# Layer 0's bias: three DMA folds to four rows a key, one sum product a group, and VectorE evicting the fourth quarter in 3 of 16 quads

## The chip, the cores and the metric

The kernel runs on one core of a Trainium2 chip. Its engines have queues of their own and meet through semaphores: TensorE (PE in the profile; PEld is its weight load), VectorE (DVE), ScalarE (ACT), GpSimd (POOL) and SyncE (SP, which here only issues DMAs). TensorE writes to PSUM, which VectorE and ScalarE can read[...]. The metric is the device time of the whole kernel in microseconds, as the median of several runs; lower is better.

## The reference

Four layers follow each other; only layer 0's attention bias matters here. For 16 groups (2 batches x 8 heads), 64 sampled keys and 1024 queries each, a small network turns the distance of query and key into one number that is added to the attention's logits:

```python
pos = grid_q[:, :, None, :] - grid_kv[:, None, :, :]
bias = jnp.sign(pos) * jnp.log1p(jnp.abs(pos))
bias = jax.nn.relu(bias @ cpb_w1 + cpb_b1)      # 2 -> 128
bias = jax.nn.relu(bias @ cpb_w2 + cpb_b2)      # 128 -> 128
bias = (bias @ cpb_w3 + cpb_b3)                 # 128 -> 1
...
sim = jnp.einsum('bhid,bhjd->bhij', qh, kh) + bias
attn = jax.nn.softmax(sim, axis=-1)
out = jnp.einsum('bhij,bhjd->bhid', attn, vh)
```

All is float32. The 16 x 64 x 1024 evaluations of the 128 x 128 product make up most of the kernel's matmul work.

## The kernel before

`layer0` walks over `quads`: `(u, o, half)` with `u` the group (0 to 15), `o` the pair of quads in it (0 to 7) and `half` 0 or 1. A quad is four keys, so 16 quads make a group's 64 keys and there are 256 quads in all. The text below calls `o` the pair.

*First hidden layer* (`first_hidden`, line 706, VectorE): for each of the four keys of a quad one tile of 128 hidden units x 1024 queries, an addition of an x part and a y part with a clamp at zero. It is issued one quad ahead, and its buffers hold two quads, so the tiles of quad i + 2 are written when TensorE is done with quad i.

*Second hidden layer* (`second_hidden`, line 730, TensorE): the 128 output units are sorted once (`sorted_weights`) so that units with like signs of `cpb_w3` stand together, and the weights' sizes are worked into the matrix. They are computed in four quarters of 32 units. A quarter's PSUM tile `hp` holds 4 keys x 32 units on its 128 partitions and all 1024 queries; three such tiles take turns. ScalarE evicts each with a bias and relu (line 740). What remains of the third layer is a sum with signs over 128 units:

- quarter 0 is multiplied by a sign per row (line 742, ScalarE), then added to quarter 1 by an accumulating DMA that GpSimd issues (line 747);
- quarter 3 += quarter 2 on GpSimd (line 751);
- quarter 3 += quarter 1 on GpSimd (line 754, in `join`, which runs during the next quad after its line 747).

That leaves 32 rows a key. Two quads share one tile `both` (`two_tiles`, three buffers). A first DMA fold (line 756, in `join` after the pair's second quad) adds odd rows to even ones: 16 rows a key. A second one (line 766, `refold`) leaves 8 rows a key; it runs in the second quad of the next pair, ahead of line 751. Right behind it SP copies (line 768) gather the rows of four quads in a tile of 16 keys x 8 rows (`sum`, three buffers). Two such tiles hold half a group; one product with a matrix of signs (`twice_product`, line 786, TensorE) sums the rows of both and puts 32 keys into the PSUM tile `sim`. It comes after pairs 5 and 1, two pairs after the last of its rows was computed. The last half group is treated apart, with one fold or none, to end early.

After a group's second product come its attention steps (`attend`): the keys' product (line 812), softmax on VectorE and ScalarE, and the values' product. The next pair of heads' preparation (`offsets`, `sampled`) is started at pair 1 of even groups. Both are generators: after each quad one step of attention runs, and, unless that step takes the turn for itself, one step of preparation.

The order on TensorE, ScalarE, VectorE and GpSimd is the order in which the loop issues (`manual_schedule`): for quad i the first layer of quad i + 1, the second layer of quad i with its evictions, then the steps.

Of the kernel before, what the change touches and what calls it, by code (L numbers as in the profile page):

```python
# [11 lines left out]
F32 = mybir.dt.float32  # L12
AF = mybir.ActivationFunctionType
ALU = mybir.AluOpType
# [21 lines left out]
    ("index", 1), ("row", 1), ("twelves", 8),  # L36
# [12 lines left out]
N_TWICE, N_FOLDED, N_SINGLE = 48, 56, 60  # L49
# [7 lines left out]
class Net:  # L57
# [40 lines left out]
    def layer0(self):  # L98
# [3 lines left out]
        with ExitStack() as ctx:  # L102
# [44 lines left out]
            with self.tc.manual_schedule(engines=engines):  # L147
# [39 lines left out]
                self.join, self.refolds, summed, group, sums = None, [], None, [], []  # L187
                for i, (u, o, half) in enumerate(quads):
                    self.half = half
                    if o == 1 and half == 1 and u % 2 == 0 and u // 2 + 1 < BP:  # L190
                        nxt = pairs[u // 2 + 1]
                        front += [self.offsets(nxt, u // 2 + 1, ps), self.sampled(nxt, u // 2 + 1, ps)]
                    h1 = ready
                    if i + 1 < len(quads):
                        if quads[i + 1][1:] == (7, 0) and u + 1 < 2 * BP:
                            self.advance(front, lambda: "logs" in pairs[(u + 1) // 2])
                        ready = self.first_hidden(*quads[i + 1], pairs, tables)
                    last_set = i >= len(quads) - 8
                    if half == 0:
                        if i + 2 < len(quads):  # L200
                            both = self.two_tiles(f"h2_{u}_{o}3")
                            group.append([both[:, 0, :], both[:, 1, :], both])
                        else:
                            group.append([self.four_rows(f"h2_{u}_{o}{n}3") for n in range(2)])
                        if o % 4 < 2 and not last_set:
                            sums.append(self.four_rows(f"sum{u}_{o}"))
                    self.second_hidden(i, u, o, half, h1, group[-1], i + 1 == len(quads), last_set)
                    if half == 1 and not last_set:
                        self.refolds.append((i + 2, group[-1][2], sums[o % 2], o % 4 // 2))
                    if half == 1 and o % 4 == 1 and summed:  # L210
                        v, e, zs = summed
                        self.twice_product(v, e, zs, sims, ps_s)
                        summed = None
                        if e == 1:
                            if v == 8:
                                self.advance(after, lambda: False)
                                att = [apool.tile([P, N], F32, tag=f"att{t}", name=f"att{v}_{t}") for t in range(CT)]
                            self.advance(front, lambda: "v" in pairs[v // 2])
                            after.append(self.attend(v, pairs[v // 2], sims.pop(v), att, ps))
                            if v % 8 == 7:  # L220
                                after.append(self.projection(ps, att, ow, v // 8))
                    elif half == 1 and o % 4 == 3:
                        if last_set:
                            self.folded_product(u, o - 2, group[:2], sims)
                        else:
                            summed, group, sums = (u, o // 4, sums), [], []
                    if not self.step(after):
                        self.step(front)

                self.join(True)  # L230
                self.advance(after, lambda: False)
                self.folded_product(u, o, group[2:3], sims)
# [35 lines left out]
    def sorted_weights(self, keep):  # L268
# [8 lines left out]
        self.places = self.spare[:, 3 * P : 4 * P + N_TWICE + N_FOLDED + N_SINGLE]  # L277
# [13 lines left out]
        many = keep.tile([P, 8], F32, tag="many", name="sort_many")  # L291
        vec.tensor_tensor(many, self.colr("twelves", 8), total.to_broadcast([P, 8]), ALU.is_le)
        vec.tensor_reduce(c["groups"], many, AX.X, ALU.add)
        vec.tensor_scalar(c["late"], c["groups"], 12.0, None, ALU.mult)
        vec.tensor_scalar(c["rest"], c["groups"], -12.0, 96.0, ALU.mult, ALU.add)
# [16 lines left out]
        signed = keep.tile([P, N_TWICE + N_FOLDED + N_SINGLE], F32, tag="signed", name="signed")  # L312
        pool.tensor_scalar(signed, self.places[:, P:], c["sign"], 1.0, ALU.mult, ALU.mult)
        self.twice = signed[:, 0:N_TWICE]
        self.folded = signed[:, N_TWICE : N_TWICE + N_FOLDED]
        self.single = signed[:, N_TWICE + N_FOLDED :]
# [15 lines left out]
        nc.scalar.copy(self.magb, small)  # L332
        self.flip = keep.tile([P, 1], F32, tag="flip", name="flip")
# [383 lines left out]
    def second_hidden(self, i, u, o, half, h1, one, final, last_set):  # L717

        nc = self.nc
        ys = []
        for q in range(4):
            hp = self.ps_h.tile([P, N], F32, tag="ps", name=f"hp_{u}_{o}{half}{q}")
            for h in range(2):
                cut = slice(h * HF, (h + 1) * HF)
                for k in range(4):
                    rows = slice(32 * k, 32 * k + 32)
                    nc.tensor.matmul(  # L730
                        hp[rows, cut], lhsT=self.l0w2[:, 32 * q : 32 * q + 32], rhs=h1[k][:, cut], start=True, stop=True
                    )
            if q < 3:
                y = self.hid2.tile([P, N], F32, tag=f"h2{q}", bufs=(2, 3, 2)[q], name=f"h2_{u}_{o}{half}{q}")
            else:
                y = one[half]
                if self.refolds and self.refolds[0][0] <= i:
                    self.refold(*self.refolds.pop(0)[1:])
            ys.append(y)
            nc.scalar.activation(y, hp, AF.Relu, bias=self.magb[:, q, 0:1])  # L740
            if q == 0:
                nc.scalar.activation(y, y, AF.Copy, scale=self.flip)  # L742
            elif q == 1:
                if final:
                    nc.vector.tensor_tensor(y, y, ys[0], ALU.add)
                else:
                    nc.gpsimd.dma_start(y, ys[0], accum_op=ALU.add)  # L747
                if self.join:
                    self.join(final)
            elif q == 3:  # L750
                (nc.vector if final else nc.gpsimd).tensor_tensor(y, y, ys[2], ALU.add)  # L751

        def join(final, z=ys[3], other=ys[1], fold=half == 1 and not final):
            (nc.vector if final else nc.gpsimd).tensor_tensor(z, z, other, ALU.add)  # L754
            if fold:
                nc.gpsimd.dma_start(one[2][0::2], one[2][1::2], accum_op=ALU.add)  # L756
                if last_set:
                    nc.sync.dma_start(one[0][1::2, :], one[1][0::2, :])

        self.join = join  # L760

    def refold(self, both, to, second):


        nc = self.nc
        nc.gpsimd.dma_start(both[0::4], both[2::4], accum_op=ALU.add)  # L766
        for half in range(2):
            nc.sync.dma_start(to[2 * second + half :: 4, :], both[0::4, half, :])

    def twice_product(self, u, e, zs, sims, ps_s):  # L770

        if u not in sims:
            sims[u] = ps_s.tile([P, HF], F32, tag="sim", name=f"sim{u}")
        at = 16 - 16 * e
        self.sum_product(u, self.twice[:, at : at + 32], e == 0, zs, sims)

    def folded_product(self, u, o, group, sims):
        at = 24 - 4 * (o - o % 2)  # L780
        self.sum_product(u, self.folded[:, at : at + 32], False, [one[0] for one in group], sims)

    def sum_product(self, u, lhsT, start, zs, sims):
        for h in range(2):
            for jj, z in enumerate(zs):
                self.nc.tensor.matmul(
                    sims[u][h * NJ + jj * 32 : h * NJ + jj * 32 + 32, :],
                    lhsT=lhsT,
                    rhs=z[:, h * HF : (h + 1) * HF],
                    start=start,  # L790
                    stop=False,
                )
# [1245 lines left out]
def _places():  # L2038

    q, row = np.arange(P) // 32, np.arange(P) % 32  # L2040
    got = np.zeros((P, P + N_TWICE + N_FOLDED + N_SINGLE), np.float32)
    got[:, :P] = np.where(q == 0, 96 + row, 12 * (row // 4) + 4 * (q - 1) + row % 4)
    p = np.arange(P)
    got[p, P + 16 + 8 * (p // 2 % 2) + 4 * (p % 2) + p // 32] = 1
    got[p, P + N_TWICE + 24 + 4 * (p % 2) + p // 32] = 1
    got[p, P + N_TWICE + N_FOLDED + 28 + p // 32] = 1
# [3 lines left out]
def _layout(i):  # L2050
# [10 lines left out]
    def over(v):  # L2061
# [13 lines left out]
        "row": (np.arange(P) % 32 // 4).astype(np.float32).reshape(P, 1), "twelves": over(np.arange(12, 108, 12, dtype=np.float32)),  # L2075
# [46 lines left out]
```

## Time and profile before

| what | value |
|---|---|
| median of 3 runs | 3223.9 us (3221.39 to 3224.66) |
| the profiled execution | 3223.45 us, its span 3221.7 us |
| bias stage, first to last start of line 730 | about 23 to 1902 us of the span |
| granted TensorE clock | 1.00 in every stretch |
| line 706, VectorE, first layer | 1020 of 128x1024, 1215 ns each |
| line 742, ScalarE, sign of quarter 0 | 256, 1152 ns each |
| line 747, GpSimd issue of the accumulating DMA | 255, 1080 ns each |
| lines 756 and 766, GpSimd issues of the folds | 127 of 859 ns, 124 of 1134 ns |
| line 768, SP copies, issue to landing | 248 of 128 KB, 3.5 us median |
| line 786, TensorE, sum products | 260 matmul records, 248 of them from copied rows |
| DMA queue of GpSimd | 232.82 MB, 37.4% of 16 engines over the span |

The profile is of one execution. A group in it is `line engine op out<-in shapes xcount | busy us, mean ns of one | idle us just before, and what ended it`. A float32 matmul is two records, and records of different column quarters run at once, so their durations must not be added; starts and the evictions that wait for them show the pace. Time in front of a DMA's landing is not in the issuing engine's busy time.

### The profile page before, as it was taken

The page shows a single profiled execution, that of the slowest core. Times are in us where ns is not written, and L with a number is a line of the kernel's source. Part 1 is how long each engine was busy: PE and PEld are TensorE (multiplying, and loading weights), DVE is VectorE, ACT ScalarE, POOL GpSimd, SP SyncE. Part 2 cuts the span into 40 slices and gives each one's busy share as a digit, 9 for nine tenths or more (in the row PEclk, how much of TensorE's full clock was granted, in tenths as well). Part 3 has the DMA queues.
Part 4 walks back from the last instruction along what each step waited for, and adds up shares of the span by engine and source line. Part 5 has one row for each costly group of instructions (what it writes and reads, how often), then busy time and mean ns, then how long its engine had stood idle before and what let it go on. Part 6 is the DMA issues. An engine that isn't in the chain of part 4 may idle for free.

```text
span 3221.7 us, 58840 instructions
## 1 busy us (share of the span) xinstructions
PE 3206.4 (100%) x24188; PEld 1218.9 (38%) x24188; DVE 2365.0 (73%) x2746; ACT 1958.2 (61%) x2032; POOL 2359.2 (73%) x1558
## 2 busy tenths in 40 slices
PE   9999999999999999999999999999999999999999
PEld 4343333333333333333333334444555433455333
DVE  7778788778777778878777765475475689755897
ACT  7887887887886687887887752112231566213662
POOL 6999999999998699998999964442343458634575
PEclk9999999999999999999999999999999999999999
DMA  6787877787786577777787762111000000000001
GB/s 178 163 172 158 171 168 163 166 167 165 162 172 145 124 164 161 163 163 164 163 174 160 166 166 79 39 40 39 1 1 12 29 1 1 15 1 14 1 2 54
DMA packets 94350, 341.90 MB, mean 106 GB/s; under 512 B 16624, under 2 KB 18800, under 8 KB 78896
## 3 DMA queue, kind: packets, MB, share of 16 engines
q0 software_dynamic: 52832, 232.82, 37.4%
q1 hardware_dynamic: 40224, 103.06, 10.0%
q8 instruction: 195, 3.19, 0.4%
q10 hardware_dynamic: 1008, 2.08, 0.2%
q14 instruction: 91, 0.75, 0.1%
HBM read 67.36 MB, written 4.46 MB: 22 GB/s over the span
## 4 chain that ended last, share of the span: by engine, by line
PE 90%; DVE 5%; POOL 2%; DMA 1%; issue 1%; ACT 0%; DVEq 0%; SPq 0%; POOLq 0%; ACTq 0%
PE hp L730 52%; PE s L1659 5%; PE o L1688 5%; PE qk20P L1434 2%; PE qk30P L1434 2%; PE qk31P L1434 1%; PE m_7P L943 1%; PE m_6P L943 1%; PE m_4P L943 1%; PE m_3P L943 1%; PE m_0P L943 1%; PE qk21P L1434 1%; PE m_5P L943 1%; PE m_2P L943 1%; PE m_1P L943 1%; DVE sum L1675 1%
## 5 line engine op out<-in xcount | busy, mean ns | idle before, releaser
L730 PE MATMUL hp<-h,w2s 128*32 128x512 f32 x16384 | 1784.1, 593 | 0.2
L706 DVE CUSTOM_DVE_ANT_1 h<-tx,bank 128x1024 f32<-128x1024 f32 (+1 forms) x1028 | 1180.9, 1211 | 295.7 <-PE hp L730 197.6
L740 ACT ACTIVATE h<-hp,magb 128x1024 f32<-128x1024 f32 x1024 | 1131.2, 1109 | 359.6 <-PE hp L730 357.7
L730 PEld LDWEIGHTS hp<-h,w2s 128*32 128x32 f32 x16384 | 559.3, 110 | 1187.0 <-issue 1126.4
L754 POOL TENSOR_TENSOR h<-h,h 128x1024 f32<-128x1024 f32 x254 | 728.2, 2867 | 2.4 <-DMA h<-h 2.3
L751 POOL TENSOR_TENSOR h<-h,h 128x1024 f32<-128x1024 f32 x255 | 717.4, 2814 | 1.5 <-ACT h L740 1.5
L1663 ACT ACTIVATE e<-s 128x1024 f32<-128x1024 f32 x256 | 261.8, 1024 | 181.0 <-PE s L1659 176.5
L747 POOL DMA_DIRECT2D h<-h x255 | 275.4, 1080 | 99.6 <-ACT h L740 97.7
L742 ACT ACTIVATE h<-h,flip 128x1024 f32<-128x1024 f32 x256 | 295.0, 1152 | 8.4
L1688 PE MATMUL o<-e,v 64*64 64x512 f32 x2048 | 265.3, 590 | 2.1 <-DVE q L1727 2.1
L1659 PE MATMUL s<-q,k 64*64 64x512 f32 x2048 | 266.0, 591 | 0.0
L1670 POOL TENSOR_TENSOR some<-some,e 128x1024 f32<-128x1024 f32 x64 | 167.6, 2619 | 26.7 <-ACT e L1663 24.1
L1668 POOL TENSOR_TENSOR some<-e,e 128x1024 f32<-128x1024 f32 x32 | 76.1, 2377 | 141.4 <-DVE sum L1677 106.3
L766 POOL DMA_DIRECT2D h<-h x124 | 140.6, 1134 | 27.0 <-DMA h<-h 24.6
L1675 DVE TENSOR_TENSOR sum<-sum,e 128x1024 f32<-128x1024 f32 x64 | 124.0, 1937 | 29.5 <-ACT e L1663 26.8
L913 POOL TENSOR_TENSOR mlp_w<-mlp_w 128x512 f32<-128x512 f32 x16 | 24.2, 1514 | 160.4 <-DMA mlp_w<-in_mlp_w 96.0
L756 POOL DMA_DIRECT2D h<-h x127 | 109.1, 859 | 38.9 <-POOL h L754 37.2
L1688 PEld LDWEIGHTS o<-e,v 64*64 64x64 f32 x2048 | 77.9, 133 | 144.9 <-issue 135.1
L1659 PEld LDWEIGHTS s<-q,k 64*64 64x64 f32 x2048 | 76.5, 133 | 133.2 <-issue 117.2
L1009 ACT ACTIVATE mh<-mh,cols 128x512 f32<-128x512 f32 x64 | 46.0, 721 | 124.4 <-DVE mh L1027 64.3
L1422 POOL TENSOR_TENSOR sq<-q 128x512 f32<-128x512 f32 x32 | 33.2, 1039 | 98.0 <-DVE q L1441 54.3
L1673 DVE TENSOR_TENSOR sum<-e,e 128x1024 f32<-128x1024 f32 x32 | 80.8, 2524 | 32.0 <-ACT e L1663 32.0
(583 smaller groups left out, 3254.4 us busy)
## 6 DMA issues: line engine op xcount, KB each, us to landing
h<-h POOLq DMA_DIRECT2D x382, 512.0 KB, 5.6
lb<-logs SPq DMA_DIRECT2D x63, 512.0 KB, 6.5
h<-h POOLq DMA_DIRECT2D x124, 256.0 KB, 3.7
sum<-h SPq DMA_DIRECT2D x248, 128.0 KB, 3.5
mlp_w<-in_mlp_w SPq DMA_DIRECT2D x16, 1024.0 KB, 4.9
x<-in_x SPq DMA_DIRECT2D x8, 512.0 KB, 7.8
qkw<-in_l_qk SPq DMA_DIRECT2D x2, 2048.0 KB, 7.9
out<-x SPq DMA_DIRECT2D x15, 256.0 KB, 2.1
```

The lines of the kernel that those rows point to most:

```text
L706: self.nc.vector._custom_dve(TENSOR_ADD_SAT, out=h1[r][:, k, cut, :], in0=x[:, 4 * half + 2 * r + k, :].unsqueeze(1).to_broadcast([P, H // ...
L730: nc.tensor.matmul(hp[rows, cut], lhsT=self.l0w2[:, 32 * q : 32 * q + 32], rhs=h1[k][:, cut], start=True, stop=True)
L740: nc.scalar.activation(y, hp, AF.Relu, bias=self.magb[:, q, 0:1])
L742: nc.scalar.activation(y, y, AF.Copy, scale=self.flip)
L747: nc.gpsimd.dma_start(y, ys[0], accum_op=ALU.add)
L751: (nc.vector if final else nc.gpsimd).tensor_tensor(y, y, ys[2], ALU.add)
L754: (nc.vector if final else nc.gpsimd).tensor_tensor(z, z, other, ALU.add)
L943: self.nc.tensor.matmul(acc[p], lhsT=w[:, a, k, p * P : (p + 1) * P], rhs=right(r, k), start=k == 0, stop=k == 1)
L1434: nc.tensor.matmul(acc, lhsT=left[0][a][:, c, t * P : (t + 1) * P], rhs=r[ri][:, c, :], start=c == 0, stop=c == 1)
L1659: nc.tensor.matmul(s[halves[c], par, :], lhsT=ks[p][rows, at : at + DH], rhs=qs[p][rows, cut], start=True, stop=True)
L1663: nc.scalar.activation(e, s, AF.Exp, scale=DH**-0.5)
L1688: nc.tensor.matmul(o[halves[par], r, :], lhsT=v[n // 2][rows, n % 2, at : at + DH], rhs=e[rows, par, :], start=(n == 0), stop=(n == NB - 1),)
```

## The change

The accumulation of each pair gets a third fold, so that four rows a key are left; the gathered tile then holds 32 keys x 4 rows, and one product of two tiles serves a whole group (`thrice`) where two products served it before. The folds and copies of a pair become a generator, `refold`, that is advanced once a quad: the second fold in the quad where it was before (now in `join`, behind line 754's add), the third fold a quad later in the same place, ahead of the next pair's first fold, and the copies at the end of the quad after that. The product stands after pair 2 of the next group; `attend` and the start of the next preparation move from pair 1 to pair 2 with it. In the last group the first half keeps two folds and its product of eight rows a key (`twice`), and what follows is as before. The sort of the units uses shares of 24 in place of 12, so that the eight rows of each of three quarters that now meet in one sum have one sign.

In quads with `fused` (second quads of pairs 1, 2, 5 and 6 of odd groups, and of pairs 1 and 3 of even groups but group 0: 46 of 256) VectorE takes the fourth quarter from PSUM, in one instruction: `max(hp, -b) + quarter 2`. This stands in place of ScalarE's eviction and GpSimd's addition. As `relu(hp + b)` is `max(hp, -b) + b`, the bias `b` is still to be added; it goes into the sign multiplication of quarter 0 as its bias (`Identity` in place of `Copy`).

```diff
-                self.join, self.refolds, summed, group, sums = None, [], None, [], []
+                self.join, self.refolds, sums, last = None, [], [], 2 * BP - 1
...
-                    if o == 1 and half == 1 and u % 2 == 0 and u // 2 + 1 < BP:
+                    if o == 2 and half == 1 and u % 2 == 0 and u // 2 + 1 < BP:
...
-                    last_set = i >= len(quads) - 8
+                    last_set = u == last and o >= 4
                     if half == 0:
+                        if o == 0:
+                            before, sums = sums, []
...
-                        if o % 4 < 2 and not last_set:
+                        if o < 2:
                             sums.append(self.four_rows(f"sum{u}_{o}"))
...
-                        self.refolds.append((i + 2, group[-1][2], sums[o % 2], o % 4 // 2))
...
+                        self.refolds.append((i + 2, i + (3 if u == last else 4), self.refold(group[-1][2], sums[o % 2], o // 2, u == last)))
+                    if half == 1 and o == 2 and u > 0:
+                        v = u - 1
+                        sims[v] = ps_s.tile([P, HF], F32, tag="sim", name=f"sim{v}")
+                        self.sum_product(sims[v], self.thrice, True, before)
...
+                    elif half == 1 and u == last and o == 5:
+                        sims[u] = ps_s.tile([P, HF], F32, tag="sim", name=f"sim{u}")
+                        self.sum_product(sims[u], self.twice[:, 16:48], True, sums)
+                    elif half == 1 and u == last and o == 7:
+                        self.sum_product(sims[u], self.folded[:, 8:40], False, [one[0] for one in group[:2]])
+                    self.refold_more(i, True)
                     if not self.step(after):
                         self.step(front)
...
+        self.under = keep.tile([P, 1], F32, tag="under", name="under")
+        pool.tensor_scalar(self.under, self.magb[:, 3, 0:1], -1.0, 1.0, ALU.mult, ALU.mult)
...
+        fused = half == 1 and u > 0 and o in ((1, 3), (1, 2, 5, 6))[u % 2] and not final
...
-                if self.refolds and self.refolds[0][0] <= i:
-                    self.refold(*self.refolds.pop(0)[1:])
             ys.append(y)
+            if q == 3 and fused:
+                vec.scalar_tensor_tensor(y, hp, self.under, ys[2], ALU.max, ALU.add)
+                continue
             nc.scalar.activation(y, hp, AF.Relu, bias=self.magb[:, q, 0:1])
-            if q == 0:
+            if q == 0 and fused:
+                nc.scalar.activation(y, y, AF.Identity, scale=self.flip, bias=self.magb[:, 3, 0:1])
+            elif q == 0:
                 nc.scalar.activation(y, y, AF.Copy, scale=self.flip)
...
-        def join(final, z=ys[3], other=ys[1], fold=half == 1 and not final):
-            (nc.vector if final else nc.gpsimd).tensor_tensor(z, z, other, ALU.add)
+        def join(final, now, z=ys[3], other=ys[1], fold=half == 1 and not final):
+            (vec if final else pool).tensor_tensor(z, z, other, ALU.add)
+            self.refold_more(now)
             if fold:
-                nc.gpsimd.dma_start(one[2][0::2], one[2][1::2], accum_op=ALU.add)
+                pool.dma_start(one[2][0::2], one[2][1::2], accum_op=ALU.add)
...
-    def refold(self, both, to, second):
+    def refold_more(self, i, gather=False):
+
+        going = []
+        for at, last, fold in self.refolds:
+            if at <= i and gather == (at == last):
+                for _ in fold:
+                    going.append((at + 1, last, fold))
+                    break
+            else:
+                going.append((at, last, fold))
+        self.refolds = going
+
+    def refold(self, both, to, c, once):
...
         nc.gpsimd.dma_start(both[0::4], both[2::4], accum_op=ALU.add)
+        if not once:
+            yield
+            nc.gpsimd.dma_start(both[0::8], both[4::8], accum_op=ALU.add)
+        yield
+        n = 4 if once else 8
         for half in range(2):
-            nc.sync.dma_start(to[2 * second + half :: 4, :], both[0::4, half, :])
...
+            nc.sync.dma_start(to[2 * c + half :: n, :], both[0::n, half, :])
```

## The prediction

> **What bounds the kernel now.** I read the engine shares, busy time by stage, the groups of instructions, and the order of time around one product.
>
> ```profile
> PE 3206.4 (100%) x24188; PEld 1218.9 (38%) x24188; DVE 2365.0 (73%) x2746; ACT 1958.2 (61%) x2032; POOL 2359.2 (73%) x1558
> ...
> 300.00:500.00 200.00, 200.00 (x1888) 64.15 (x1880) 158.94 (x173) 164.48 (x161) 187.35 (x125) 1.00 0.79 166
> ...
> L730 PE MATMUL hp<-h,w2s 128*32 128x512 f32 x16384 | 1784.1, 593 | 0.2
> L740 ACT ACTIVATE h<-hp,magb 128x1024 f32<-128x1024 f32 x1024 | 1131.2, 1109 | 359.6 <-PE hp L730 357.7
> L754 POOL TENSOR_TENSOR h<-h,h 128x1024 f32<-128x1024 f32 x254 | 728.2, 2867 | 2.4 <-DMA h<-h 2.3
> L751 POOL TENSOR_TENSOR h<-h,h 128x1024 f32<-128x1024 f32 x255 | 717.4, 2814 | 1.5 <-ACT h L740 1.5
> ```
>
> The second line is a 200 us stretch of the bias stage (busy PE, PEld, DVE, ACT, POOL, then granted clock, DMA share, GB/s). TensorE is busy 200.00 of 200, GpSimd 187.35, VectorE 158.94. Line 730 waited 0.2 us in all, while ScalarE waited 357.7 us for it: evictions are early, TensorE sets the pace. [...] I checked the pace by start times:
>
> ```profile
> 341.63 1.11 ACT L740 ACTIVATE h<-hp,magb 128x1024 f32<-128x1024 f32 x1 [0.56 <-PE hp L730]
> 344.18 1.12 ACT L740 ACTIVATE h<-hp,magb 128x1024 f32<-128x1024 f32 x1 [1.44 <-PE hp L730]
> ...
> 349.36 1.11 ACT L740 ACTIVATE h<-hp,magb 128x1024 f32<-128x1024 f32 x1 [0.56 <-PE hp L730]
> 351.05 1.12 ACT L740 ACTIVATE h<-hp,magb 128x1024 f32<-128x1024 f32 x1 [0.58 <-PE hp L730]
> ...
> 356.22 1.11 ACT L740 ACTIVATE h<-hp,magb 128x1024 f32<-128x1024 f32 x1 [0.57 <-PE hp L730]
> ...
> 341.36 1.04 PE L786 MATMUL sim<-sum,signed 128*32 128x512 f32 x8
> ```
>
> From fourth quarter to fourth quarter a quad takes 356.22 - 349.36 = 6.86 us; the one after the sum product of line 786 takes 349.36 - 341.63 = 7.73 us, and its first eviction waits 1.44 instead of 0.58 us. So a product costs TensorE 0.86 us, all on the path. The starts of line 730 over the stage agree: quads with nothing else average 6.886 us (171 of them, shortest 6.863), those with a product 7.725 (14).
>
> [...] line 766's DMA issue, which doesn't wait for the add before it, starts 0.35 us (median) before that add ends; line 756, which does, 0.30 us after it. [...] line 375, the form of the new VectorE instruction (PSUM, column, SBUF; 128x1024), takes 1.284 us. [...] no table load stands at the Identity of line 458, so the new one adds none.
>
> **The change part by part.**
>
> *Products.* Before there are 31 of eight rows a key (248 matmul records at line 786, eight each); after, 15 of four rows a key (groups 0 to 14) and one of eight (group 15's first half). The last group's other products stay. 15 x 0.859 = 12.9 us off TensorE, all on the path.
>
> *VectorE evicts the fourth quarter* in 4 quads of odd groups and 2 of even ones: 8 x 4 + 7 x 2 = 46. ScalarE loses 46 x 1.11 = 51 us, GpSimd 46 x 2.81 = 129 us; VectorE gains 46 x 1.28 = 59 us and has 20% idle, so the sum fits. The place is what matters. The new instruction waits for the end E of its quad's matmuls; queued behind it are the iteration's steps (softmax, offsets, sampling), which used to run before E, and the four first-layer tiles of the quad after next, which waited for E already (their buffers). Those take 4.61 us in the timeline and are due at E + 6.87. With 0.06 for the semaphore (my allowance): 0.06 + 1.28 + 4.61 = 5.95, so 0.9 us of cover. In VectorE's order 31 of the 46 have no step there: nothing. The other 15 (pairs counted from 0):
> - Group 10, pair 3: a subtract of 0.68 and the batch norm of 1.88: 8.51, so 1.6 us late.
> - Group 9, pair 1: a reduce of 1.49: 0.55 late.
> - Groups 2, 4, 6, 8, 12, pair 3: a subtract of 0.68 and two query copies of 0.69: 8.0, but TensorE runs the query matmuls there (1.13), so they are due at 8.0; I take 0.1 each.
> - Eight with small copies or one subtract, 0.7 or less: inside the cover.
> Together 2.7 us. Bounds: -3 (the 171 plain quads hold 171 x 0.023 = 4 us of small delays that may shrink as steps move) and +10 (0.2 in each of the 46, if ScalarE's third quarter or a semaphore comes later). The PSUM tile is freed at E + 1.35 instead of E + 1.17 and wanted at E + 3.4: nothing.
>
> *Third fold.* One more GpSimd DMA issue for each pair of groups 0 to 14: 120, an operation that the trace lacks. Nearest row: line 766, 1.134 us. It stands behind the join add, ahead of the first fold. It can start inside the add's tail as line 766 does, behind which the next add starts 0.25 us (median) after the last: so 0.25 to 1.13 a pair; I take 0.5, 60 us, less than the 129 that GpSimd loses. Where VectorE doesn't help (five pairs in a row, nine at the start) the high end adds 9 x 1.13 = 10.2 us against idle time of (200 - 187.35) / 29 quads = 0.44 each, 7.9: a lag of 2.3 us. ScalarE's third-quarter buffer, which the fourth-quarter add frees 6.4 us after its quad (362.63 against 356.2), is wanted 12 us after it: hidden. The fold waits for the second's landing (3.7 us), issued a quad (6.87) before: no wait as a rule. Its bytes, 120 x 128 KB, are what the copies lose (240 of 128 KB become 64).
>
> *Copies one quad later.* This eats cover. A row buffer (three, one a pair) is free when its copies have landed, and ScalarE's fourth quarter three pairs on rewrites it. From the issue records of line 768 and the evictions, that margin is 10.6 us before (median of 120; the smallest 2.9, 4.5, 5.3, 6.5, 7.1). The third fold takes 6.87 us of it. A median of 3.8 remains, and ScalarE may be 2.2 us late before TensorE runs out of its three PSUM tiles (3.4 - 1.17). By the same list four pairs fall short, by 4.0, 2.4, 1.6 and 0.4: over 2.2 that is 1.8 + 0.2 = 2.0 us. Smaller copies land earlier; I take 1.5. Bounds: 0, and 8 if GpSimd's lag of 2.3 comes on top (ten pairs more within 0.8 us of the edge). The product itself, at the sixth quad of the next group, has some 9 us after the last copies: hidden.
>
> *Attention steps* move by a pair with the product, their work unchanged. *Prologue*: one more 128x1 GpSimd operation, other constants: 0 to 0.2, I take 0.
>
> Sum on the profiled execution (3223.45 us: span 3221.7 and 1.75 around it): -12.9 + 2.7 + 1.5 = -8.7, so 3214.75. The median of the runs is 0.45 higher: 3215.2. I say 3215.
>
> **The rivals.**
> - *VectorE's place eats the gain.* For: 46 times a waiting instruction stands ahead of tiles that TensorE needs, with 0.9 us of cover, and VectorE's tiles wait 31.3 + 28.4 us today for ScalarE's use of the shared PSUM bank. Against: ScalarE has less to do in just these quads. If each costs another 0.19 us: 46 x 0.19 = 8.7, no change, 3224.
> - *The row buffers bind (slower).* Three buffers turn in three pairs, 41.2 us. Where the round takes e longer than that and the 2.2 us, every pair takes e / 3 longer: 120 x e / 3 = 40 e. The margin of the median is 3.8 + 2.2 = 6.0; the rival decides from 6.0 + 0.2 us of further delay. For: DMA engines busy 0.79, second folds that landed as late as 6.4 us, GpSimd's lag of 2.3, SP's copies up to 12.5 us after the fold's landing where SP waits for something else. With 2.7 + 2.3 + 2 = 7.0: 40 us of stall against 8.7: 3255. Against: they would have to come together in nearly every pair.
> - *More than the sum.* Group 10 finds cover and the small delays shrink: 3223.9 - 12.9 - 1 = 3210.
> - GpSimd as the bound needs (129 + 118 idle) / 120 = 2.06 us a fold, twice the issue: I give it nothing of its own.
>
> **How the numbers follow.** Forecast 0.62, VectorE's place 0.16, row buffers 0.12, more than the sum 0.10. About 0.2% (6.4 us) tells from no change here, so below 3217.5 is faster: of the forecast 0.54, of VectorE's place 0.03, and 0.10: 0.67. Within: 0.08 + 0.11 + 0.02 = 0.21. Slower: 0.02 + 0.10 = 0.12. The range runs from 3209.5 (more than the sum) to 3224 (VectorE's case, or the high bound of one unknown cost: 3215 + 8); the row buffers' case stays outside.
>
> **What would show it.** Right: 128 matmul records of sum products where 248 were; plain quads at 6.87 us, also those that VectorE evicts; GpSimd a little less busy; one longer quad in group 10. Wrong: evicted quads of 7.1 us or more, TensorE waiting for first-layer tiles; ScalarE waiting for the copies or GpSimd (0.4 us today for GpSimd); waits ahead of the third fold.

## The result and the profile after

The changed kernel takes 3281.02 us in the median of 4 runs (3271.84 to 3281.85), the kernel before 3223.85 us beside it; the ratio is 1.0172 (95% interval 1.0153 to 1.0191). The change made the kernel slower by 57 us, where 9 us less were forecast. The profiled execution took 3281.85 us, its span 3280.1.

These are the lines of its page that answer to those of before (busy us, mean ns of one, then the idle time ahead of the group and what ended it), with two groups that are new:

```profile
PE 3216.7 (98%) x24068; PEld 1223.2 (37%) x24068; DVE 2421.0 (74%) x2792; ACT 1911.4 (58%) x1986; POOL 2339.6 (71%) x1633
...
L739 PE MATMUL hp<-h,w2s 128*32 128x512 f32 x16384 | 1804.7, 599 | 48.0 <-ACT h L750 47.7
...
L750 ACT ACTIVATE h<-hp,magb 128x1024 f32<-128x1024 f32 x978 | 1078.6, 1109 | 430.7 <-PE hp L739 326.8
...
L766 POOL TENSOR_TENSOR h<-h,h 128x1024 f32<-128x1024 f32 x254 | 759.8, 2991 | 4.5 <-DMA h<-h 4.5
L763 POOL TENSOR_TENSOR h<-h,h 128x1024 f32<-128x1024 f32 x209 | 642.8, 3076 | 34.8 <-ACT h L750 25.2
...
L794 POOL DMA_DIRECT2D h<-h x120 | 149.5, 1246 | 0.0
...
L748 DVE SCALAR_TENSOR_TENSOR h<-hp,under,h 128x1024 f32<-128x1024 f32 x46 | 59.0, 1284 | 97.8 <-ACT h L750 70.5
```

The second layer (line 739, line 730 of before) waited 0.2 us for anything before; now it waits 48.0 us, nearly all of it for ScalarE's eviction. ScalarE and GpSimd are less busy than before, VectorE more, as forecast. No engine has become the bound by its busy time: work waits. The stages show the same (after: busy PE, PEld, DVE, ACT, POOL, then granted clock, DMA share, GB/s):

```profile
100.00:300.00 200.00, 199.90 (x1876) 64.35 (x1869) 161.20 (x167) 156.79 (x152) 187.87 (x132) 1.00 0.86 169
300.00:500.00 200.00, 191.25 (x1756) 60.67 (x1748) 157.81 (x176) 152.45 (x150) 175.35 (x125) 0.97 0.79 156
```

The first 300 us run as before. From then on TensorE stands still for 4 to 9 us in each stretch of 200 up to 1900 us, and its clock is no longer granted in full.

To see how much, I took the 256 quads by the starts of line 739, and gave each kind of quad (with nothing else, with keys, with values, with a product and so on) the shortest duration that it has in the trace of before. The sum of these is what the stage would take without a stall, and the rest is excess. Before: 1860.6 us and 10.8 of excess. After: 1847.7 and 81.3. So the work of the path fell by 12.9 us (a figure priced with the trace of before) and the stalls rose by 70.5; together +57.6, against +58.4 between the two profiled executions. The excess isn't spread: eleven quads are 4.5 to 7.9 us too long, all but one of them second quads of pairs 0 and 4 of odd groups, and most of the others, evicted by VectorE or not, take their 6.87 us.

What these quads wait for is in the view of waits, here for the stage from 100 to 1900 us (us in total, times, longest). After:

```profile
ACT h L750 <- DMA sum<-h: 75.7, 18, 8.1
...
PEld hp L739 <- ACT h L750: 73.9, 43, 6.3
...
PE hp L739 <- ACT h L750: 47.7, 12, 5.4
```

Before, ScalarE has no such line; of TensorE's two there is one:

```profile
PEld hp L730 <- ACT h L740: 5.2, 13, 0.5
```

So ScalarE can't write the row buffer `both`, because the copies that read it (`sum<-h`) haven't landed, and TensorE runs out of PSUM tiles behind it. One such place on ScalarE's timeline of after (start, us, and in brackets the idle time before it with what ended it):

```profile
373.57 1.12 ACT L750 ACTIVATE h<-hp,magb 128x1024 f32<-128x1024 f32 x1 [0.19 <-PE hp L739]
380.80 2.12 ACT L750 ACTIVATE h<-hp,magb 128x1024 f32<-128x1024 f32 x2 [6.12 <-DMA sum<-h]
```

and SP's queue at the same place (the number behind the start is the time from the first issue of the line to its last):

```profile
356.73 1.79 SPq L798 DMA_DIRECT2D sum<-h  x2
374.75 0.37 SPq L653 DMA_DIRECT2D lb<-logs  x1
375.28 9.49 SPq L798 DMA_DIRECT2D sum<-h  x4
```

The copies that ScalarE waits for go out at 375.28 us. Their third fold was issued at 364.84 and landed 4.5 us later, at 369.3: from then on the rows were ready, and the copies were held for 5.9 us. In SP's queue a table load (line 653, line 646 of before) stands ahead of them. It refills a buffer that VectorE's line 698 has still to read, and SP waited in its semaphore from 358.6 to 374.7 us, until that read at 374.2. Before, the copies stood ahead of the load:

```profile
362.93 14.09 SPq L768 DMA_DIRECT2D sum<-h  x4
377.11 0.54 SPq L646 DMA_DIRECT2D lb<-logs  x1
```

Over the whole span SP waits for that read, after and then before:

```profile
SPq L653 <- DVE bank L698: 487.1, 54, 33.5
```

```profile
SPq L646 <- DVE bank L691: 64.6, 28, 17.6
```

The order on SP is not written out: `manual_schedule` names PE, ScalarE, VectorE and GpSimd, and SP's DMAs are placed by a scheduler. To see how often copies were held, I took for each pair of quads the time from the landing of its last fold to the issue of its first copy. Before, it is 0.4 us at most in all 124 pairs. After, 107 of 120 pairs go out within 0.6 us, and 13 are held for 3.8 to 8.5. Eleven of these 13 are the pairs whose buffers the eleven long quads need.

In seven of the 13 the table load has come ahead of the copies, as above; all seven are in even groups. In the other six, pair 1 of five odd groups and pair 4 of group 9, it is the loads that prepare the next pair of heads (lines 461, 466 and 569; in group 9 with table loads among them). Those stood ahead of the same copies in the kernel before, too, but were through in time. Group 3, after:

```profile
429.41 0.34 SPq L461 DMA_DIRECT2D logs<-log  x1
431.59 0.34 SPq L466 DMA_DIRECT2D spots<-g  x1
435.66 0.32 SPq L569 DMA_DIRECT2D at<-spots  x1
436.20 1.13 SPq L798 DMA_DIRECT2D sum<-h  x2
```

and before:

```profile
414.05 0.34 SPq L454 DMA_DIRECT2D logs<-log  x1
414.51 1.15 SPq L459 DMA_DIRECT2D spots<-g  x1
422.06 0.32 SPq L562 DMA_DIRECT2D at<-spots  x1
422.56 13.23 SPq L768 DMA_DIRECT2D sum<-h  x4
```

Before, the fold landed at 422.2, just behind the last of these loads. After, it landed at 429.1, ahead of the first, which SP could issue only when VectorE had made its data (line 459). The preparation starts a pair later in the changed program. These six pairs are behind the larger part of the loss, 44.5 us of the 72 in the eleven quads. SP's wait for that data over the span is 78.9 us after (7 times) and 33.3 before (6 times).

Which part of the change made the scheduler move the table loads was not settled. The delay of the copies alone did not (e9_copies_at_once below), and VectorE's evictions alone left the order of before (e2_evict_only: no pair held over 0.4 us). No run moved the preparation back by itself either. What the order costs is plain in the place shown above: for 16.2 us SP issued nothing, although the copies behind the load had been ready for the last 5.4 of them.

### The profile page after: what moved, and what is told of

The parts are those of the page before. It is cut to its first block, busy times and chain, and to the rows that moved or that the text cites. A ratio compares the mean times of both kernels' runs of the same rounds, so it can differ in the third digit from the quotient of the medians.

```text
span 3280.1 us, 58877 instructions
## 1 busy us (share of the span) xinstructions
PE 3216.7 (98%) x24068; PEld 1223.2 (37%) x24068; DVE 2421.0 (74%) x2792; ACT 1911.4 (58%) x1986; POOL 2339.6 (71%) x1633
## 4 chain that ended last, share of the span: by engine, by line
PE 80%; POOL 8%; DVE 6%; DMA 3%; issue 2%; ACT 1%; SPq 0%; DVEq 0%; POOLq 0%; ACTq 0%
PE hp L739 42%; PE s L1679 5%; PE o L1708 5%; POOL h L766 3%; POOL h L763 2%; DMA sum<-h 2%; PE qk20P L1454 1%; PE qk30P L1454 1%; PE qk31P L1454 1%; PE qk21P L1454 1%; PE m_7P L963 1%; PE m_5P L963 1%; PE m_4P L963 1%; PE m_2P L963 1%; PE m_0P L963 1%
## 5 line engine op out<-in xcount | busy, mean ns | idle before, releaser
L739 PE MATMUL hp<-h,w2s 128*32 128x512 f32 x16384 | 1804.7, 599 | 48.0 <-ACT h L750 47.7
L750 ACT ACTIVATE h<-hp,magb 128x1024 f32<-128x1024 f32 x978 | 1078.6, 1109 | 430.7 <-PE hp L739 326.8
L739 PEld LDWEIGHTS hp<-h,w2s 128*32 128x32 f32 x16384 | 567.5, 111 | 1249.9 <-issue 1114.7
L766 POOL TENSOR_TENSOR h<-h,h 128x1024 f32<-128x1024 f32 x254 | 759.8, 2991 | 4.5 <-DMA h<-h 4.5
L763 POOL TENSOR_TENSOR h<-h,h 128x1024 f32<-128x1024 f32 x209 | 642.8, 3076 | 34.8 <-ACT h L750 25.2
L759 POOL DMA_DIRECT2D h<-h x255 | 326.7, 1281 | 178.5 <-ACT h L750 176.7
L754 ACT ACTIVATE h<-h,flip 128x1024 f32<-128x1024 f32 x210 | 241.7, 1151 | 6.9
L791 POOL DMA_DIRECT2D h<-h x124 | 161.8, 1305 | 11.7 <-DMA h<-h 7.9
L769 POOL DMA_DIRECT2D h<-h x127 | 163.9, 1290 | 4.5 <-issue 2.4
L794 POOL DMA_DIRECT2D h<-h x120 | 149.5, 1246 | 0.0
L748 DVE SCALAR_TENSOR_TENSOR h<-hp,under,h 128x1024 f32<-128x1024 f32 x46 | 59.0, 1284 | 97.8 <-ACT h L750 70.5
```

Of the source, the lines that this page charges most:

```text
L739: nc.tensor.matmul(hp[rows, cut], lhsT=self.l0w2[:, 32 * q : 32 * q + 32], rhs=h1[k][:, cut], start=True, stop=True)
L759: pool.dma_start(y, ys[0], accum_op=ALU.add)
L763: (vec if final else pool).tensor_tensor(y, y, ys[2], ALU.add)
L766: (vec if final else pool).tensor_tensor(z, z, other, ALU.add)
```

## The experiments

Four theories. A: the order of SP's queue holds the copies back. B: VectorE's evictions stall TensorE (the prediction's first rival). C: GpSimd, with a third fold in each pair, is the bound. D: the copies' designed delay of one quad eats the margin of the row buffers, in whatever order. Each run stood beside runs of the kernel before (medians 3221.5 to 3221.8 us). The last column is the number of pairs whose copies SP held for over 1 us, as counted above; it is 13 in the change and 0 before.

| run | what it is | median us | ratio to before, 95% | held |
|---|---|---|---|---|
| e1_no_evict | the change without VectorE's evictions | 3359.84 | 1.0424 (1.0406 to 1.0441) | 24 |
| e2_evict_only | before with VectorE's evictions alone | 3238.55 | 1.0053 (1.0037 to 1.0070) | 0 |
| e4_sp_order | the change with SP in the program's order | 3223.40 | 1.0006 (0.9997 to 1.0015) | 0 |
| e5_act_copies | the change, copies on ScalarE's queue | 3234.15 | 1.0037 (1.0023 to 1.0051) | not on SP |
| e6_sp_tail | e4 with earlier copies in the last group | 3223.96 | 1.0006 (0.9998 to 1.0015) | 1 |
| e7_sp_no_evict | e6 without VectorE's evictions | 3242.94 | 1.0066 (1.0051 to 1.0082) | 1 |
| e9_copies_at_once | the change without the copies' delay | 3274.06 | 1.0161 (1.0145 to 1.0177) | 13 |
| e8_sp_tail2 | e6 with its one bad place put right | 3214.21 | 0.9976 (0.9966 to 0.9986) | 0 |
| e11_before_sp | before with SP in the program's order | 3232.24 | 1.0035 (1.0022 to 1.0049) | 0 |

**VectorE's evictions: taken out of the change, and alone.**

```diff
-        fused = half == 1 and u > 0 and o in ((1, 3), (1, 2, 5, 6))[u % 2] and not final
+        fused = False
```

> The third fold with its copies and products as in the change, but no quad is evicted by VectorE. Theory A (SyncE's queue: table loads that wait for VectorE, and the chain of logs and spots, stand ahead of the copies; row buffers come free late, ScalarE and then TensorE wait): the order of SyncE's queue is the same as in the change, so the long waits of ScalarE for copies stay, 60 to 90 us of them, and the time is 3265 to 3295. Theory B (the new VectorE instruction stands ahead of tiles that TensorE needs): 3208 to 3218. Theory C (the third fold overloads GpSimd): GpSimd gets 129 us of additions back, so 3300 or more.

Measured 3359.84 us, 79 us worse than the change and 65 above what A expected; it lies where C expected it. The wait of the change grows, in the same view:

```profile
ACT h L750 <- DMA sum<-h: 119.5, 21, 8.8
```

B falls, as the evictions help. Between A and C this run can't decide, because SP's order is not that of the change, although the expectation took it to be. The scheduler set more table loads ahead of copies: 24 pairs are held instead of 13, and the excess is 164.4 us instead of 81.3. How much of the 79 us is that order and how much GpSimd's extra work, this run doesn't show; e7_sp_no_evict below asks with the order fixed.

The other half of this pair, the evictions put into the kernel before with nothing else (the edit is the `fused` part of the change's diff):

> The kernel before with VectorE evicting the fourth quarter in the 46 quads, and nothing else of the change. Theory A: no long wait of ScalarE for copies; no product is saved; up to 3 us for VectorE's place: 3222 to 3230. Theory B: 3260 to 3290. Theory C: GpSimd is relieved and nothing is added: 3218 to 3226.

Measured 3238.55 us, 17 slower than before. No theory's range holds it; A's ended at 3230. The excess of the stage is 25.2 us against 10.8, and over half of the new part lies in six quads that come after an evicted one and take an attention step: those with the values' product in pair 4 of even groups, 1.4 us each. So the place of the evictions among VectorE's steps seems to count, in the old places of the steps. In the change the steps are a pair later, and the quads with the values' product exceed by 0.3.

**SP's order.** The change with SP named in `manual_schedule`. So that the table load has time to land (6.5 us in the median of before), it is issued a pair earlier in the program (its use stays where it was), and so that its data is there, the preparation of the next pair of heads is brought to the point where its logs are made one pair earlier too.

```diff
-            engines = {getattr(mybir.EngineType, e) for e in ("PE", "Activation", "DVE", "Pool")}
+            engines = {getattr(mybir.EngineType, e) for e in ("PE", "Activation", "DVE", "Pool", "SP")}
...
-                        if quads[i + 1][1:] == (7, 0) and u + 1 < 2 * BP:
+                        if quads[i + 1][1:] == (6, 0) and u + 1 < 2 * BP:
...
+            tables["coming"] = got, f"tx{u}{c}"
+
+        def spread():
+            got, name = tables.pop("coming")
...
             tables["logs"], tables["x"] = tables.pop("next")
+            if u < 2 * BP - 1 or o < 6:
+                load(*((u, o // 2 + 1) if o < 6 else (u + 1, 0)))
         elif u < 2 * BP - 1 or o < 7:
-            load(*((u, o // 2 + 1) if o < 7 else (u + 1, 0)))
+            spread()
```

> The change, with SyncE's DMAs in the order of the program and each table load issued one pair of quads earlier in it (two after the last read of its buffer), so that no copy stands behind a load that waits for VectorE. Theory A: the waits of ScalarE for copies go to under 10 us in all, the granted clock to 1.00, the time to 3209 to 3219. Theory B and C: 3265 or more, nothing of theirs is changed.

Measured 3223.40 us: the 57 us are back, though 4 above the upper end of what A expected. SP holds no pair's copies any more, and where pair 1's copies had stood behind the preparation's loads, they now go out ahead of them. The waits for 100 to 1900 us:

```profile
ACT h L756 <- DMA sum<-h: 9.6, 6, 2.1
...
PE sim L812 <- DMA sum<-h: 5.0, 1, 5.0
```

The first was 75.7 us. The second is new: the last sum product itself waits, in group 15, where the copies of pair 3 stand behind a fold that SP issues for pair 4 (line 777), and one quad is 7.4 us too long.

**The copies alone, past SP's queue.** They are issued by ScalarE's queue; the order of SP's loads stays.

```diff
-            nc.sync.dma_start(to[2 * c + half :: n, :], both[0::n, half, :])
+            nc.scalar.dma_start(to[2 * c + half :: n, :], both[0::n, half, :])
```

> The change, with the copies of the folded rows issued from ScalarE's queue at their place in the program (end of the second quad after the third fold), and all else on SyncE. Theory A: no copy waits behind a table load; ScalarE pays two issues a pair, some 120 us of its idle time, and may evict late now and then: 3210 to 3228. Theory B and C: 3265 or more.

Measured 3234.15 us. 47 us are back by moving the copies alone, as A says. The upper end of A's expectation is missed by 6. Its 120 us are 0.5 us for each of 240 issues; on SP one took 0.53 us in the median of after (line 798). From 100 to 1900 us the view of waits puts 55 us of ScalarE's idle time to `issue`, where it names no release, and none in the change. That ScalarE waited there for the folds' landing, before it could issue a copy, is a guess; no view shows it. The excess of 34.8 us is spread, 27.6 of it over quads with nothing else in them, by at most 1 us in nearly all.

**The delay alone.** The change with the copies issued in the quad of their third fold, SP left to the scheduler.

```diff
-                        self.refolds.append((i + 2, i + (3 if u == last else 4), self.refold(group[-1][2], sums[o % 2], o // 2, u == last)))
+                        self.refolds.append((i + 2, -1, self.refold(group[-1][2], sums[o % 2], o // 2, u == last)))
...
-        yield
         n = 4 if once else 8
```

> The change with its copies issued in the same quad as the third fold, without the quad's delay; SP's order is left to the scheduler, and puts the table load ahead of pair 5's copies in even groups, and the logs, spots and index loads ahead of pair 1's copies in odd groups. Theory A (SP's order): the stalls move to those pairs and stay, 3255 to 3285. Theory D (the delay of one quad is what eats the margin, as the prediction's row-buffer rival has it): the copies go out some 6 us earlier, and the time is 3225 or less, 3212 to 3225.

Measured 3274.06 us, in A's range. D falls, and with it the form that the prediction gave to the row-buffer rival: without the delay the loss stays. ScalarE's wait for the copies in the stage, and SP's waits over the span:

```profile
ACT h L750 <- DMA sum<-h: 64.1, 15, 7.7
```

```profile
SPq L653 <- DVE bank L698: 490.2, 54, 35.2
...
SPq L461 <- DVE log L459: 80.2, 7, 13.9
```

The load's wait is that of the change, and the same 13 pairs are held. The quads that stall are also the same, pairs 0 and 4 of odd groups, so here the expectation that they would move was not met.

**The last group.** e4 with the copies of the last group issued right behind their fold, in the program's order.

```diff
-                        self.refolds.append((i + 2, i + (3 if u == last else 4), self.refold(...)))
+                        self.refolds.append((i + 2, -1 if u == last else i + 4, self.refold(...)))
...
-        yield
+            yield
```

> The change with SP in the program's order and the table load issued one pair earlier (as e4_sp_order), and in the last group alone the copies issued right behind their fold instead of a quad later. Theory A (the loss of the change is the order of SP's queue): e4_sp_order left one long quad, the last product of group 15 at 7.4 us over its nominal, whose copies stood behind a fold that was waiting; without it 3223.4 - 7 = about 3216, between 3212 and 3219, below before. Theory C (GpSimd with a third fold in every pair is the bound, whatever SP's order): the tail's order makes no difference, 3221 to 3226. Theory D (the copies' designed delay of one quad is what costs): no difference either, since only the last group's delay is taken away, 3220 to 3226.

Measured 3223.96 us, the same as e4: A's number was missed, and the ranges of C and D hold it. The long quad of pair 5 is gone, but one of pair 2 of group 15 is 7.2 us too long instead. SP's timeline there:

```profile
1795.02 0.53 SPq L653 DMA_DIRECT2D lb<-logs  x1
1816.79 16.50 SPq L804 DMA_DIRECT2D sum<-h  x6
```

The edit had put the copies of group 15's first pair ahead of those of group 14's last pair. The latter were ready first (their third fold landed at 1808.54), and went out at 1818.11, behind the others, which waited for a fold that landed at 1816.64. It is the only pair held in this run, and the mechanism of the change again, made by hand.

The next kernel keeps the quad's delay for that one pair (the edit against e6_sp_tail, its lines shortened):

```diff
-(i + 2, -1 if u == last else i + 4, self.refold(..., u == last))
+(i + 2, i + 4 if u < last else i + 3 if o == 0 else -1, self.refold(..., u == last, u == last and o > 0))
...
-    def refold(self, both, to, c, once):
+    def refold(self, both, to, c, once, soon):
...
+        if not soon:
             yield
```

> As e6_sp_tail, but the copies of the last group's first pair a quad later again, so that they stand behind the copies of group 14's last pair: in e6_sp_tail they stood ahead of those, SP waited for their fold until 1816.8 us, and one quad was 7.2 us long. Theory A (the loss is the order of SP's queue): the 7.2 us go and none come in their place, 3216.5, between 3213 and 3219, a ratio under 0.9985. Theory C (GpSimd's work is the bound whatever SP's order): another quad takes the 7 us, 3221 to 3226.

Measured 3214.21 us, inside A's range and outside C's; it beats both kernels. From its page, then the same 200 us as above, and ScalarE's wait from 100 to 1900 us:

```profile
L745 PE MATMUL hp<-h,w2s 128*32 128x512 f32 x16384 | 1783.9, 593 | 5.3 <-ACT h L756 3.7
```

```profile
300.00:500.00 200.00, 199.89 (x1888) 65.60 (x1884) 169.17 (x187) 159.82 (x157) 187.91 (x135) 1.00 0.86 168
```

```profile
ACT h L756 <- DMA sum<-h: 6.5, 5, 2.1
```

TensorE's idle time ahead of the second layer is 5.3 us instead of 48.0, and the clock is whole. The excess is 18.7 us: -12.9 + (18.7 - 10.8) = -5.0, and the profiled executions of this kernel and of before differ by 3218.40 - 3223.45 = -5.05. (The profiled execution is the slowest of this kernel's nine, 4.2 above their median.)

**Is SP's order a gain of its own?** The kernel before, with the edits of e4_sp_order:

> The kernel before with the two edits of e4_sp_order alone: SP in the program's order and the table load issued one pair earlier. Theory A: before has no copies that stand behind a waiting load, so there is nothing to win back; 3219 to 3227. The rival, that SP's order is a gain of its own and would have helped before as well, so that e4_sp_order says nothing of the change's loss: 3165 to 3200.

Measured 3232.24 us: a loss of 10.7 us, more than A expected, and the opposite of a gain. What e4 and e8 win is therefore the change's own loss. With the same edits in both, the change is worth 3223.4 - 3232.2 = -8.8 us; e8 is 18 us below e11, but it carries a further edit to the last group that e11 doesn't have. Of the 10.7 us, 6.7 are excess in the stage, most of it in pairs 6 and 7 of group 9 and pair 3 of group 10; why there was not tried.

**GpSimd by itself.** e6 without VectorE's evictions, so that GpSimd has all adds and the third folds, with SP in order.

> As e6_sp_tail, with VectorE's evictions left out: the fourth quarter is added by GpSimd in all 16 groups. Without VectorE's help e1_no_evict was at 3360. Theory A: with SP in order GpSimd's later folds don't turn into stalls; 3215 to 3228. Theory C: GpSimd falls behind by 0.4 us a pair over the 120 pairs with nothing to catch up on, and the row buffers pass it on: 3250 to 3290, many waits of ScalarE for the copies, all the later ones of a group. In between (3228 to 3250): both.

Measured 3242.94 us, between A's range and C's, where the expectation put "both": 19 us above e6, with the same one pair held in both. The stretch from 100 to 900 us, in this kernel and then in the kernel before:

```profile
100.00:900.00 800.00, 791.86 (x7379) 249.59 (x7375) 627.91 (x689) 637.88 (x626) 779.16 (x540) 1.00 0.84 165
```

```profile
100.00:900.00 800.00, 799.98 (x7488) 259.99 (x7484) 636.77 (x703) 650.15 (x634) 748.19 (x488) 1.00 0.79 166
```

By the starts of the second layer these are 110.38 and 111.07 quads, so GpSimd is busy 14.12 us a pair instead of 13.47: the third fold costs it some 0.65 us. GpSimd is busy 97% of the time, and 14.12 us is more than the 13.73 of two quads with nothing else in them. So C is a part of the truth: by this estimate GpSimd falls behind by 0.4 us in such pairs without VectorE's help. With the help it isn't the bound, since e8 reaches the forecast. The same evictions are worth 19 us with SP in order and 79 without, but in the second figure SP's order differs too (24 pairs held against 13).

A fourth row buffer, which would also separate the copies from ScalarE, was not tried.

## Why the prediction was wrong

**The step that failed is "Copies one quad later",** and in it the sentence that took the margin from the records of line 768 of before and subtracted one quad. That takes for granted that the copies go out when their last fold has landed, as they did before, by 0.4 us at most. In the changed program SP held 13 pairs' copies for 3.8 to 8.5 us: seven behind table loads that the scheduler had set ahead, six behind the preparation's loads, which went out later against the rows. Of the steps that move by a pair the prediction says only "their work unchanged"; what SP's queue does with the DMAs that move with them its sum put at nothing, without a reason. The smallest margins of its list were a sign: of the five that it names, four (2.9, 4.5, 5.3 and 7.1) belong to pairs right behind these loads.

I allowed 1.5 us, with 8 as the upper bound; the stage's stalls grew by 70.5, and 57 us of the time went away when SP's order and the place of its loads were put right (e4), 47 when only the copies left SP (e5). Leaving out the delay that the step did price gave back 7 (e9). Two smaller terms of the step are off as well. 10.6 less 6.87 is 3.7, not 3.8. And the smaller copies did not land earlier in the change: 4.1 us in the median against 3.5 before (3.1 in e8).

**The row-buffer rival** named the right resource, and then asked for a common cause in nearly every pair. It is enough that a load stands ahead of the copies in a few places: eleven quads of 4.5 to 7.9 us. So its time, 3255, was too low and its chance too small. One of the prediction's own signs of being wrong is what came: ScalarE waiting for the copies, 75.7 us. The rival's "SP's copies up to 12.5 us after the fold's landing where SP waits for something else" came near the wait but misread it: in group 9 of before those copies went out 0.4 us after the fold had landed, and then took 11 us to land.

**Products**: -12.9 forecast. The sum of the quads gives the same, but by construction, as it prices each quad with the trace of before. What the trace of after adds: line 806 has 128 matmul records where line 786 had 248, and the second quads of pair 5, which lost a product, take the time of their kind within 0.3 us.

**VectorE's place**: 2.7 forecast, about nothing found. The instruction took 1.284 us, as read from line 375 of before. The 0.06 us for the semaphore was an allowance; line 375 started 0.04 us after the end of the matmul that released it. The new `Identity` brought no table load of ScalarE with it: there are 30 in the trace of before and 30 in that of after. Group 9's pair 1 and group 10's pair 3 run at their nominal time in the trace of after. e2 suggests that what decides is which step follows the eviction: with the steps left where they were, the evictions cost 17 us.

**Third fold**: 0.5 us a pair forecast inside bounds of 0.25 to 1.13; e7 gives 0.65. That GpSimd as the bound got no chance of its own was right for the change as made, but only because of the 46 evictions.

**The sum**: with SP in order the same parts give 3214.2 us (e8), where the forecast was 3215. That doesn't prove each term: e8 carries SP's edits too, which cost the kernel before 10.7 us, and an edit to the last group. That these come out so close to the forecast is partly luck.

## What to carry to other kernels

A change that moves a DMA, or a step that makes a DMA's data, must be followed in the order of every queue, also one whose order nobody has written out: list SP's DMAs before and after, and look for what stands ahead of the ones on the path, what that waits for, and when it goes out. Here the order was new for seven of the thirteen held pairs and old for six. One prefetch that was hoisted early held SP's queue for 16.2 us, until its buffer was free, and the copies behind it, ready for the last 5.4 of them, waited too; it belonged behind the transfers that free a buffer on the path. A margin read from a trace holds only for the order and the times in which that trace was made. And an edit that looks as if it left a queue alone can change its order, as e1 did: count it again in every run.

## What was not expected of the hardware

The long stalls of TensorE cost more than their length. These are the windows around the stall shown above, in the profile of after (columns as in the stages):

```profile
378.00:381.95 3.95, 0.59 (x8) 0.00 (x0) 1.80 (x2) 1.15 (x2) 3.07 (x3) 0.92 1.00 232
381.95:385.00 3.05, 3.03 (x16) 0.80 (x20) 0.00 (x0) 3.02 (x3) 3.00 (x2) 0.55 0.98 201
385.00:393.00 8.00, 8.00 (x80) 2.28 (x76) 5.10 (x5) 7.11 (x9) 6.66 (x5) 1.00 0.56 112
```

After a pause of 3.4 us the clock granted over the next 3 us is 0.55 in the mean: three rounds of four matmuls start 0.85 us apart instead of 0.43, then the pace is whole again. The clock records of the trace have eleven such spells in the stage, each at one half and 3.41 or 6.83 us long, one at each of the eleven long quads.

At these quads TensorE had stood still for 2.59 us (before 1854.6) to 5.37 us (before 445.9). After the next shorter pause in the stage, 1.05 us before 1824.4, the records show the whole clock.

After the eleven stalls 49 rounds are slow in this way, which costs 49 x 0.42 = 21 us. That is 0.6% of the span, and yet over a quarter of the 70.5 us of stalls. The prediction's price of a stall, its length alone, was too low by that share.
